# Random features in row and column groups, local layers by slots of both key tiles, offsets on VectorE

## The chip, the core and the metric

The kernel runs on one NeuronCore of a Trainium2 chip. TensorE (PE; its weight loads are listed as PEld) multiplies matrices into PSUM, VectorE (DVE), ScalarE (ACT) and GpSimd (POOL) do the work by elements, and SyncE (SP) issues most DMAs. PSUM has eight banks of 128 partitions by 512 f32 values. Every engine takes its instructions in the order in which the program issued them, and waits for the others at semaphores. The metric is the device time of one execution in microseconds (us); less is better.

## The reference

A network of 16 blocks on a stream x of 16 x 256 tokens with 128 channels, all in f32; each block adds its result to x. The change concerns blocks 2, 3 and 4. Blocks 2 and 4 are the same local attention with two layers, block 3 is an attention by random features (a performer). What they compute, with `_layernorm(x)` ahead of each:

```python
# local attention, one of two layers (8 heads of 64, windows of 64 tokens, 341 hidden)
q, k, v = split(shift_token(x) @ wqkv)
q, k = rotary_xpos(l2norm(q) * qs, l2norm(k) * ksc)
mask = (i < j) | (i > j + WINDOW) | (j == -1)
o = softmax(where(mask, -max, 8 * q @ k.T)) @ v
x = x + o @ wo
h = norm(shift_token(x)) * lg + lb
a, g = split(h @ w1 + b1)
x = x + (a * gelu(g)) @ w2 + b2

# performer (16 heads of 8, 32 random features per head)
def phi(u):
    proj = u @ omega.T
    return exp(proj - 0.5 * sum(u * u) - max(proj)) / sqrt(32) + 1e-6
pq, pk = phi(q * 8**-0.25), phi(k * 8**-0.25)
num, den = pq @ (pk.T @ v), pq @ sum(pk)
x = layernorm(x + (num / den) @ wo) * ln1_g + ln1_b
x = layernorm(x + gelu(x @ w1 + b1) @ w2 + b2) * ln2_g + ln2_b
```

## The kernel before

Activations stay in SBUF with channels on the partitions: x, and two work tiles ha and hb, each 128 x 4096. A chunk is 512 tokens (eight chunks), a tile is 128 tokens (32 tiles), and two tiles are one batch of 256 tokens. Steps are written out by hand: a loop over slots calls each step's function for the tile or chunk that is due, and within one engine the instructions stand in the order of these calls. PSUM banks are handed out by tag, with a fixed number for each tag; a new use of a bank waits for the readers of the old one. The helpers mm, act, tt, gt, stt and ts (lines 503 to 543) issue one instruction each, so most rows of the profile carry a helper's line: L504 is a matmul, L508 a transpose, L528 ScalarE, L531, L538 and L543 VectorE, L534 GpSimd. A matmul in f32 is issued as two instructions on TensorE, a transpose as one.

**Local attention, attend** (`local_attend`, line 3360, called once in each of the four local layers). For a tile n, `project` makes q and k in two banks with tag "w" (tokens on the partitions); ScalarE squares both, VectorE multiplies both by tables of cosines and sines into t1 and t2. `rotate` sums the squares by head (VectorE) and adds the halves (GpSimd), `unit` takes the inverse root with a logarithm and an exponential (ScalarE) and multiplies (GpSimd). `turn` transposes to qkt with heads of 64 channels on the partitions and makes v. `score` works on a unit (batch b, half hg of the heads, key tile t): four f32 matmuls with 64 contracted rows into two banks "s". With t = 0 the 192 columns of queries that see the key tile are limited by a minimum against the table "see" (VectorE) and raised in one exponential of 128 x 768; with t = 1 a mask is first put into the banks by a bf16 matmul of the identity (256 columns), and ScalarE raises straight from PSUM. `weigh` follows two units later: twelve f32 matmuls with 32 output rows each, four side by side in the partitions, first the denominators pd (weights are ones) and then the values po, both in banks "o", summed over t. After t = 1 ScalarE makes the inverse rd of pd by a logarithm and an exponential, and `divide` multiplies (VectorE). `out` multiplies a chunk by wo. The banks are w=3, s=2, o=3, and the loop runs over units, two per slot of a tile.

`chunk_steps` adds, by chunk: the norm of x (centre, spread, scale; first layers only, and only for the three chunks that the block before has not normed), `shift` by one token on GpSimd, and the norm of the shifted z in hs, in the banks "w". A norm centres with a matmul (`centre_step`, line 1759: copy by ScalarE, square by GpSimd) and then makes the variance with a second matmul, a logarithm and an exponential (`spread_step`, line 1774). `norm_steps` (line 1791) returns the three steps; with g and b given, the scale step is a multiply on VectorE and an offset on ScalarE (line 1807).

**Local attention, feed-forward** (`local_ffn`, line 3551): for each chunk six wide matmuls with gelu, then three narrow ones; banks f=6, z=2. In the second layer of a block, steps of the next block's norm follow in the banks "z".

**Performer** (`performer_attend`, line 2249; all eight banks have the tag "ps"). `project` makes q and k of a chunk with channels on the partitions, ScalarE scales, GpSimd squares. `lengths` sums the squares by head, `values` makes v. `features` works on a tile: for each of q and k one matmul of 128 x 128 by the block-diagonal w["om"] (128 x 512), a maximum by head and the subtraction on VectorE, one exponential of 128 x 1024 on ScalarE, one scaling on GpSimd. `turn` transposes the features of q, `sums` makes pk.T @ v of a batch and masks it with own and own1, `heads` multiplies a tile (four f32 matmuls of 36 columns), with a reciprocal and a product on VectorE, `join` transposes the result of a chunk back, `out` multiplies by wo and adds, and `end` is the norm with ln1_g and ln1_b. The list `steps` gives each step's slot; a batch passes from features to heads in slots 0 to 5. `performer_ffn` (line 2381) follows, with the second norm.

Of the kernel before, what the change touches and what calls it, by code (L numbers as in the profile page):

```python
# [1649 lines left out]
class Fast(Net):  # L1650
# [140 lines left out]
    def norm_steps(self, pool, src, dst, bank, g=None, b=None, eps="eps5", copy=None, square=False):  # L1791
# [10 lines left out]
        def scale():  # L1802
            if g is None:
                self.tt(dst, dst, held[1], ALU.mult)
            else:
                self.stt(dst, dst, g, held[1], ALU.mult, ALU.mult)
                self.act(dst, dst, AF.Identity, bias=b)
# [441 lines left out]
    def performer_attend(self, w):  # L2249


        nc = self.nc
        h0, y = self.ha, self.hb
        s8 = 8.0**-0.25
        with ExitStack() as st:
            p = self.stage(st, "f2", 1)
            qk, nrm, vs, fs, kvs, fts, os, ots, ends = {}, {}, {}, {}, {}, {}, {}, {}, {}
# [12 lines left out]
            def lengths(c):  # L2270
                pn = self.bank()
                for side in range(2):
                    for t in range(4):
                        at = (2 * t + side) * 16
                        self.mm(pn[:, at : at + 16], qk[c, side][1][:, t * P : t * P + P], w["half"])
                nrm[c] = p.tile([P, 4, 2, 16], F32, tag="nrm", name="nrm", bufs=2)
                nc.vector.tensor_copy(nrm[c].rearrange("p t s h -> p (t s h)"), pn[:, :P])
# [10 lines left out]
            def features(n):  # L2288
                c, t = divmod(n, 4)
                f = p.tile([P, 2, 16, 32], F32, tag="f", name="f", bufs=6)  # L2290
                sub = p.tile([P, 2, 16], F32, tag="sub", name="sub", bufs=2)
                pps = []
                for side in range(2):
                    pp = self.bank()
                    self.mm(pp, qk[c, side][0][:, t * P : t * P + P], w["om"])
                    pps.append(pp.rearrange("p (h m) -> p h m", h=16))
                for side in range(2):
                    nc.vector.tensor_reduce(sub[:, side], pps[side], AX.X, ALU.max)
                self.tt(sub, sub, nrm[c][:, t], ALU.add)
                for side in range(2):  # L2300
                    self.tt(f[:, side], pps[side], sub[:, side, :, None].broadcast_to([P, 16, 32]), ALU.subtract)
                flat = f.rearrange("p s h m -> p (s h m)")
                self.act(flat, flat, AF.Exp)
                nc.gpsimd.tensor_scalar(flat, flat, 32.0**-0.5, 1e-6, ALU.mult, ALU.add)
                fs[n] = f.rearrange("p s h m -> p s (h m)")

            def sums(b):
                pkv = self.bank()
                for g in range(4):
                    for u in range(2):  # L2310
                        n = 2 * b + u
                        self.mm(
                            pkv[:, g * 33 : g * 33 + 33], fs[n][:, 1, g * P : g * P + P], vs[n // 4][:, n % 4, g],
                            start=u == 0, stop=u == 1,
                        )
                kv = p.tile([P, 4, 36], F32, tag="kv", name="kv", bufs=2)
                pk3 = pkv[:, : 4 * 33].rearrange("p (g k) -> p g k", g=4)
                self.tt(kv[:, :, :32], pk3[:, :, :32], w["own"][:, None, :].broadcast_to([P, 4, 32]), ALU.mult)
                self.tt(
                    kv[:, :, 32:], pk3[:, :, 32:33].broadcast_to([P, 4, 4]),  # L2320
                    w["own1"][:, None, :].broadcast_to([P, 4, 4]), ALU.mult,
                )
                kvs[b] = kv

            def turn(n):
                pf = self.bank()
                for g in range(4):
                    self.tr(pf[:, g * P : g * P + P], fs[n][:, 0, g * P : g * P + P])
                ft = p.tile([P, 4, P], F32, tag="ft", name="ft", bufs=3)
                self.act(ft.rearrange("p g t -> p (g t)"), pf, AF.Copy)  # L2330
                fts[n] = ft

            def heads(n):
                ft, kv = fts.pop(n), kvs[n // 2]
                pn = self.bank()
                for g in range(4):
                    self.mm(pn[:, g * 36 : g * 36 + 36], ft[:, g], kv[:, g])
                pn3 = pn[:, :144].rearrange("p (g k) -> p g k", g=4)
                rd = p.tile([P, 4, 4], F32, tag="rd", name="rd", bufs=2)
                nc.vector.reciprocal(rd, pn3[:, :, 32:])  # L2340
                if n % 4 == 0:
                    os[n // 4] = p.tile([P, 4, P], F32, tag="o", name="o", bufs=2)
                self.tt(
                    os[n // 4][:, n % 4].rearrange("p (g h k) -> p g h k", g=4, h=4),
                    pn3[:, :, :32].rearrange("p g (h k) -> p g h k", h=4),
                    rd[:, :, :, None].broadcast_to([P, 4, 4, 8]), ALU.mult,
                )

            def join(c):
                pt = self.bank()  # L2350
                o = os.pop(c)
                for t in range(4):
                    self.tr(pt[:, t * P : t * P + P], o[:, t])
                ots[c] = p.tile([P, CH], F32, tag="ot", name="ot", bufs=1)
                self.act(ots[c], pt, AF.Copy)
# [1452 lines left out]
```

## Time and profile before

Three executions took 4376.58, 4367.05 and 4374.96 us, the median is 4374.96 us. The execution that was profiled is another one.

| what | value |
|---|---|
| profiled execution | 4392.96 us, its span 4391.2 us |
| TensorE busy, mean granted clock | 3966.2 us (90%), 0.952 |
| VectorE, ScalarE, GpSimd busy | 2605.3, 2376.1, 2119.4 us |
| attend of a local layer, first to last score matmul | 140.9 to 417.4, 519.5 to 782.4, 1198.8 to 1475.3, 1577.7 to 1841.0 us |
| performer attend, first to last subtraction of features | 883.1 to 1057.5 us |
| score matmuls (64 rows) | 2048, median 322 ns |
| products with values, with ones (32 columns of the array) | 4096 and 2048, median 300 and 312 ns |

A row of the profile gives the engine, the line, the operation, what is written and what is read, and the shape. In the answers in order of time a row begins with its start and its duration in us, and equal neighbours are merged with their count. A note in square brackets is the idle time of the engine before the row, and what ended it. Durations of matmuls overlap with their neighbours, so what an instruction costs TensorE is read from the distance of two starts.

### The profile page before, as it was taken

How to read it: one execution, taken by the hardware profiler on the slowest of the kernel's cores; microseconds unless marked ns; L12 is line 12 of the kernel's file. 1: busy time of each engine (PE TensorE's matmuls, PEld its weight loads, DVE VectorE, ACT ScalarE, POOL GpSimd, SP SyncE). 2: the span in 40 equal slices, each digit the busy share in tenths (PEclk: the TensorE clock that was granted, in tenths of full speed). 3: DMA queues.
4: the chain of work that ended last, by engine and by line, in shares of the span. 5: the costliest groups of instructions: out<-in, count | busy, mean ns of one | idle time of the engine just before them, and what ended most of it. 6: DMA issues, size and time to landing. Idle time of an engine off the chain costs nothing. (4 is left out here: it accounts for less than half of the span.)

```text
span 4391.2 us, 72802 instructions
## 1 busy us (share of the span) xinstructions
PE 3966.2 (90%) x28390; PEld 2202.4 (50%) x28390; DVE 2605.3 (59%) x4455; ACT 2376.1 (54%) x4549; POOL 2119.4 (48%) x1776
## 2 busy tenths in 40 slices
PE   7899999999899999995989969887999899899978
PEld 3455455466355445543975549643333344355333
DVE  4764566364366377456336643564888788386374
ACT  6665466444766456553447634445555554675442
POOL 4653355232455255315433334466998789521251
PEclk8999999999999999997999979998999999999989
DMA  1800000000000000001940029200000000000000
GB/s 59 332 1 1 11 1 1 19 1 1 19 1 1 1 3 1 1 0 49 310 162 10 15 88 326 86 18 16 1 1 1 3 1 1 15 2 18 6 0 20
DMA packets 78400, 176.36 MB, mean 40 GB/s; under 512 B 12606, under 2 KB 39108, under 8 KB 77920
## 3 DMA queue, kind: packets, MB, share of 16 engines
q1 hardware_dynamic: 65568, 148.40, 9.8%
q0 software_dynamic: 9120, 18.51, 1.2%
q8 instruction: 227, 3.72, 0.4%
q10 hardware_dynamic: 3360, 4.72, 0.3%
q14 instruction: 125, 1.02, 0.1%
HBM read 118.28 MB, written 54.20 MB: 39 GB/s over the span
## 5 line engine op out<-in xcount | busy, mean ns | idle before, releaser
L528 ACT ACTIVATE pt<-ps 128x512 f32<-128x512 f32 (+1 forms) x896 | 423.1, 537 | 408.1 <-PE ps L504 406.8
L504 PE MATMUL ps<-hb,w 128*128 128x512 f32 (+1 forms) x960 | 468.9, 623 | 5.4 <-issue 3.3
L531 DVE TENSOR_TENSOR t<-ps,tab 128x512 f32<-128x512 f32 x512 | 319.3, 683 | 196.1 <-ACT sq L528 191.3
L504 PE MATMUL ps<-w,hb 128*128 128x512 f32 (+2 forms) x896 | 415.1, 576 | 13.6 <-DVE t L531 11.3
L534 POOL TENSOR_TENSOR t<-t,ss 128x1024 f32<-128x1024 f32 x128 | 243.7, 1904 | 306.8 <-ACT ss L528 197.7
L534 POOL TENSOR_TENSOR t<-t,t 128x512 f32<-128x512 f32 x256 | 320.5, 1275 | 13.2 <-PE ps L504 10.1
L504 PEld LDWEIGHTS ps<-hb,w 128*128 128x128 f32 (+1 forms) x960 | 183.6, 196 | 273.5 <-issue 247.3
L531 DVE TENSOR_TENSOR u<-u,ps 128x384 f32<-128x384 f32 (+1 forms) x206 | 121.8, 595 | 277.8 <-ACT u L528 131.2
L534 POOL TENSOR_TENSOR nsq<-ha 128x512 f32<-128x512 f32 x112 | 123.2, 1100 | 314.1 <-ACT ha L528 297.3
L504 PE MATMUL ps<-nsq,ct 128*128 128x512 f32 x368 | 209.5, 654 | 53.9 <-POOL nsq L534 35.0
L528 ACT ACTIVATE pt<-pt 128x768 f32<-128x768 f32 (+1 forms) x160 | 169.5, 1060 | 154.6 <-DVE pt L531 154.6
L2199 POOL DMA_INDIRECT back<-y,x x142 | 139.1, 980 | 184.2 <-ACT y L528 90.2
L504 PE MATMUL ps<-qkt 64*128 64x192 f32 (+1 forms) x2048 | 216.2, 326 | 11.8 <-ACT pt L528 11.8
L504 PE MATMUL ps<-u,w 128*128 128x512 f32 (+1 forms) x448 | 218.8, 612 | 8.0 <-POOL u L534 8.0
L504 PE MATMUL ps<-ot,w 128*128 128x512 f32 x448 | 211.1, 604 | 15.2 <-POOL ot L534 6.9
L504 PE MATMUL ps<-xt,w 128*128 128x128 f32 x1704 | 219.8, 279 | 1.5 <-ACT xt L528 1.5
L504 PEld LDWEIGHTS ps<-qkt 64*128 64x128 f32 x2048 | 153.1, 188 | 133.3 <-ACT qkt L528 51.5
L504 PEld LDWEIGHTS ps<-w,hb 128*128 128x128 f32 x896 | 147.4, 192 | 139.4 <-issue 110.7
L531 DVE TENSOR_TENSOR pt<-ps,w 128x384 f32<-128x384 f32 (+1 forms) x320 | 171.2, 576 | 75.6 <-PE ps L504 72.2
L3705 POOL DMA_INDIRECT rows<-out,idx x128 | 126.4, 988 | 174.6 <-ACT out L528 125.6
L528 ACT ACTIVATE u<-ps,w 128x512 f32<-128x512 f32 x160 | 107.2, 685 | 186.3 <-PE ps L504 183.5
L531 DVE TENSOR_TENSOR pt<-pt,w 128x1024 f32<-128x1024 f32 (+1 forms) x96 | 181.1, 1886 | 42.3 <-ACT pt L528 42.3
(362 smaller groups left out, 9127.2 us busy)
## 6 DMA issues: line engine op xcount, KB each, us to landing
w<-in_moe_x SPq DMA_DIRECT2D x142, 533.0 KB
rows<-t SPq DMA_DIRECT2D x64, 520.0 KB
x<-rows SPq DMA_DIRECT2D x142, 65.0 KB
w<-in_local_f SPq DMA_DIRECT2D x8, 659.5 KB
y<-back ACTq DMA_DIRECT2D x16, 256.0 KB
y<-back SPq DMA_DIRECT2D x16, 256.0 KB
w<-in_local_f SPq DMA_DIRECT2D x4, 658.5 KB
back<-y,x POOLq DMA_INDIRECT x142
```

What stands on the lines that cost most here:

```text
L504: self.nc.tensor.matmul(out, lhsT, rhs, start=start, stop=stop)
L528: self.nc.scalar.activation(out, in_, func, **kw)
L531: self.nc.vector.tensor_tensor(out, a, b, op)
L534: self.nc.gpsimd.tensor_tensor(out, a, b, op)
L2199: nc.gpsimd.indirect_dma_start(views[i], bass.IndirectOffsetOnAxis(ap=x[:, C : C + 1].bitcast(I32), axis=0), y, None, bounds_check=2 * NT ...
L3705: nc.gpsimd.indirect_dma_start(views[(c * 2 + k) * 4 + t], bass.IndirectOffsetOnAxis(ap=idx[:, k, t : t + 1], axis=0), out[:, k, t], None,)
```

## The change

**Offsets.** The scale step of `norm_steps` adds b with a tensor_scalar on VectorE in place of an activation on ScalarE. It concerns the two norms of the performer, 16 instructions in all; the local layers get steps of their own, `norm_of_half`, with four steps and the offset still on ScalarE.

**Performer.** `features` works on a batch: 16 f32 matmuls of 32 rows by 128 columns, each with the four heads of one group g, into four banks with the tag "f"; the maxima of two groups, an addition and two subtractions follow, twice. `raised` is a step of its own, one slot later. `sums` makes the denominators 32 wide too, `heads` works on a batch with the features as the moving operand and 32 output rows for each group, so that `join` falls away; the reciprocal becomes a logarithm and an exponential on ScalarE. Banks are f=4, ps=4, and a batch passes from features to heads in slots 0 to 7.

**Local attend.** A slot m is a batch and a half of the heads, with both key tiles. `score` takes four banks "s": four bf16 masks of 128 columns, then the products of t = 0 and t = 1 without a change of kind between them; the 128 columns per head of t = 1 lie in a second tile pu. The last two of these are raised in `score`, the first two and the 768 columns in `first_weights`, after `turn`. `weigh` follows one slot later, values first and denominators last; the denominators lie in the upper half of the slot's fourth bank. The banks are w=3, s=4, o=1. Tiles are turned two slots ahead of their score and projected five slots ahead.

**Local feed-forward.** The norm of the last chunk moves from the end of attend into the first four chunks of `local_ffn`, with the table of the logarithm loaded before its spread step.

```diff
@@ norm_steps
-                self.act(dst, dst, AF.Identity, bias=b)
+                self.ts(dst, dst, b, ALU.add)
@@ performer_attend
+            def features(b):
...
+                pps = [self.bank("f") for _ in range(4)]
+                for u in range(2):
+                    for side in range(2):
+                        for g in range(4):
+                            rows, t = slice(32 * g, 32 * g + 32), b % 2 * 2 + u
+                            self.mm(
+                                pps[g][:, (2 * u + side) * P : (2 * u + side) * P + P],
+                                qk[c, side][0][rows, t * P : t * P + P], w["om"][rows, g * P : g * P + P],
+                            )
+                for k in range(2):
+                    gs = slice(2 * k, 2 * k + 2)
+                    for g in (2 * k, 2 * k + 1):
+                        nc.vector.tensor_reduce(sub[:, g], pps[g].rearrange("p (n m) -> p n m", m=32), AX.X, ALU.max)
+                    flat = sub[:, gs].rearrange("p g n -> p (g n)")
+                    self.tt(flat, flat, nrm[c][:, b % 2, 32 * k : 32 * k + 32], ALU.add)
+                    for g in (2 * k, 2 * k + 1):
+                        self.tt(
...
+                        )
+            def raised(b):
+                for k in range(2):
+                    flat = fs[b][:, 2 * k : 2 * k + 2].rearrange("p g u s m -> p (g u s m)")
+                    self.act(flat, flat, AF.Exp)
+                    nc.gpsimd.tensor_scalar(flat, flat, 32.0**-0.5, 1e-6, ALU.mult, ALU.add)
...
+            def heads(b):
+                ft, kv = fts.pop(b), kvs.pop(b)
                 pn = self.bank()
...
+                for k in range(2):
+                    for g in range(4):
+                        nc.tensor.matmul(pn[32 * g : 32 * g + 32, k * T : k * T + T], kv[:, k, g], ft[:, g], start=k == 0, stop=k == 1, skip_group_check=True)
+                rd = p.tile([P, T], F32, tag="rd", name="rd", bufs=2)
+                self.act(rd, pn[:, T:], AF.Ln)
+                self.act(rd, rd, AF.Exp, scale=-1.0)
...
+                self.tt(ots[b // 2][:, b % 2 * T : b % 2 * T + T], pn[:, :T], rd, ALU.mult)
...
+                (13, 4, NCH, end(2)), (12, 4, NCH, end(1)), (11, 4, NCH, end(0)), (10, 4, NCH, out),
+                (7, 2, B, heads), (5, 2, B, sums), (3, 1, NTILE, turn), (1, 2, B, raised), (0, 2, B, features),
...
+            with self.share(f=4, ps=4):
+                self.tiles_in_slots(-7, NTILE + 14, steps)
@@ local_attend
+            def score(m):
...
+                ps = [self.bank("s") for _ in range(4)]
+                for x in (*(b[:, 384:] for b in ps[:2]), *(b[:, :P] for b in ps[2:])):
+                    self.mm(x, identb, masked, stop=False)
...
+                for i, t, bank, at in ((0, 0, 0, 0), (1, 0, 0, 192), (0, 1, 0, 384), (1, 1, 2, 0)):
                     for a in range(2):
...
+                        product(a, i, t, ps[bank + a][:, at : at + 192 - 64 * t])
...
+                for a in range(2):
+                    self.act(pu[:, 2 + a], ps[2 + a][:, :P], AF.Exp)
+                weights[m] = pt, pu
+                spare[:] = ps
+
+            def first_weights(m):
+                pt, pu = weights[m]
+                for a in range(2):
+                    self.act(pu[:, a], spare[a][:, 384:], AF.Exp)
+                flat = pt.rearrange("p a t -> p (a t)")
+                self.act(flat, flat, AF.Exp)
+
+            def weigh(m):
...
+                pd, po = spare[3][:, T:] if m < NTILE - 1 else self.bank("s")[:, T:], self.bank("o")
+                pt, pu = weights.pop(m)
+                for half in (0, 1, -1):
+                    for t in range(2):
...
+            with self.share(w=3, s=4, o=1), self.tc.manual_schedule():
                 self.logs()
...
+                for m in range(-9, NTILE + 6):
+                    if within(m, NTILE):
+                        score(m)
+                    if within(m - 1, NTILE):
+                        weigh(m - 1)
+                    c, rest = divmod(m - 5, 4)
+                    if rest == 0 and 0 <= c < NCH:
                         out(c)
...
+                    if within(m + 2, NTILE):
+                        turn(m + 2)
+                    if within(m, NTILE):
+                        first_weights(m)
+                    if within(m + 4, NTILE):
+                        rotate(m + 4)
+                    if within(m - 1, NTILE):
+                        inverse(m - 1)
+                        divide(m - 1)
+                    if within(m + 4, NTILE):
+                        unit(m + 4)
+                    chunk_steps(m)
+                    if within(m + 5, NTILE):
+                        project(m + 5)
@@ local_ffn
+                end = self.norm_of_half(p, "z", w, hn[:, self.chunk(NCH - 1)])
                 for k in range(NCH + 1 + len(lead)):
                     if k < NCH:
                         wide(k)
+                    if k < 4:
+                        if k == 1:
+                            self.logs(False)
+                        end[k]()
                     if 0 < k <= NCH:
                         narrow(k - 1)
```

## The prediction

> **What bounds the kernel now.** I read the busy table first, then the slices of the span, then the order of instructions in time inside each stage that the change touches. The page's first rows:
>
> ```profile
> span 4391.2 us, 72802 instructions
> PE 3966.2 (90%) x28390; PEld 2202.4 (50%) x28390; DVE 2605.3 (59%) x4455; ACT 2376.1 (54%) x4549; POOL 2119.4 (48%) x1776
> ```
>
> TensorE is busy nine tenths of the span. Asked for the stretches: attend of the second local layer (497 to 785 us) 275.8 of 288 us, performer attend (868 to 1083 us) 204 of 215. What matters is therefore the spacing of TensorE's starts. One tile step of local attend, TensorE alone in order of time (start, duration, instruction, count):
>
> ```profile
> 263.24 0.92 PE L504 MATMUL ps<-qkt 64*128 64x192 f32 x8
> 264.09 0.53 PE L3478 MATMUL ps<-pt,ct 128*32 128x192 f32 x8
> 264.44 0.83 PE L3478 MATMUL ps<-pt,v 128*32 128x192 f32 x16
> 265.20 1.98 PE L504 MATMUL ps<-w,hb 128*128 128x512 f32 x4
> 267.02 1.02 PE L504 MATMUL ps<-hb,ct 128*128 128x512 f32 x2
> 267.88 0.38 PE L504 MATMUL ps<-masked,identb 128*128 128x256 bf16 x2
> 268.19 0.71 PE L504 MATMUL ps<-qkt 64*128 64x128 f32 x8
> 268.84 0.42 PE L3478 MATMUL ps<-pt,ct 128*32 128x128 f32 x8
> 269.08 0.62 PE L3478 MATMUL ps<-pt,v 128*32 128x128 f32 x16
> 269.63 1.09 PE L508 MATMUL ps<-ct,t 128*128 128x128 f32 x8
> 270.56 1.02 PE L504 MATMUL ps<-w,hb 128*128 128x512 f32 x2
> ```
>
> No row carries an idle note. Differences of starts: scores 0.85, sums 0.35, values 0.76, projection 1.82, centring 0.86, mask 0.31, scores 0.65, sums 0.24, values 0.55, transposes 0.93, v 0.96 us: 8.28 with the norm's matmul, 7.42 without. A 512-column f32 instruction costs 0.427 us in a run, 128 columns 0.107. At that pace the rows (pairs of 64-row and fours of 32-column tiles together) add up to 6.3 us; the other 1.1 us lies where tile shapes change: about 0.1 into the 64-row scores, 0.2 out of them, 0.12 out of the 32-column products.
>
> Where TensorE does wait: the end of each local attend, and the norm of x in a first layer (three chunks):
>
> ```profile
> 785.54 1.98 PE L504 MATMUL ps<-ot,w 128*128 128x512 f32 x4
> 788.13 1.98 PE L504 MATMUL ps<-ot,w 128*128 128x512 f32 x4 [0.61 <-DVE ot L531]
> 792.34 1.21 PE L504 MATMUL ps<-hb,ct 128*128 128x512 f32 x2 [2.23 <-POOL hb L696]
> 795.36 2.07 PE L504 MATMUL ps<-nsq,ct 128*128 128x512 f32 x2 [1.81 <-POOL nsq L534]
> 797.22 3.30 PE L504 MATMUL ps<-hb,w 128*128 128x512 f32 x4
> ```
>
> ```profile
> 251.36 1.10 PE L504 MATMUL ps<-nsq,ct 128*128 128x512 f32 x2 [2.42 <-ACT qkt L528]
> ```
>
> [...]
>
> **Local attend, a full slot (128 of them: 32 in each of 4 layers).** Six changes of tile shape become three. Masks: four of 128 columns for two of 256; loads paced at 0.1, so about 0.5 for 0.31. Scores 0.64+0.43+0.21 = 1.28 for 1.50. Products 1.60+0.15 = 1.75 for 1.90. Transposes 0.93. v 0.86 and projection 1.76, no longer followed or preceded by a change, for 2.78. Sum 7.08 for 7.42.
>
> But with all four "s" banks taken by every slot, the next slot's fourth mask needs the bank whose upper half holds the denominators, so it waits for their logarithm. In the changed order of ScalarE that stands behind the copy of v, two 128-column exponentials and the 768-column one. Counted from the start of the v matmul, with paces from ScalarE's rows in time (copy starts 1.07 later and takes 0.50, exponentials 0.16 each, worked out from 0.28 for two of 256 columns, 768 columns 0.76, logarithm 0.39, hand-over 0.1): the fourth mask can go at 3.22, the next v at 3.22+0.1+1.28+1.75+0.93 = 7.3 (R1). Behind that mask stand the scores and products, and VectorE's minima and ScalarE's exponentials wait for those. TensorE alone would be there at 7.08. A second chain (R2): after the logarithm its exponential, the two of the unit norm, the slot's norm work on ScalarE, the two squares, then the exponential of the denominators' bank, before the sums: 6.75 plus the norm work. A third (R3): first square, four VectorE multiplies (2.48), which free the bank of the next v: 7.0 plus the norm work. Behind those multiplies VectorE has the minima of the next scores (1.02 for two), which ScalarE wants only 1.6 us after the next v has begun.
>
> Norm work is 0.6 (offset), 0 plus centring 0.5, 1.2 (spread), 0 over four slots; TensorE gets 0.86 in the second and third and the output product (3.5) in the fourth. Four slots after: 7.6, 7.94, 8.2, 7.3+3.5: 34.5. Before: 4 x 7.42 + 1.72 + 3.54 = 34.9. So the steady part gains only 0.4 in four slots.
>
> **A whole layer.** From first to last score before: 519.48 to 778.73, 259.25 us. After: six early slots without norms 47.3 (five of 7.3, one 10.8), five fours 172.5, the last ones without a projection 26.0 (R1 holds them at 7.3 where before takes 5.6 from start to start), edges 9.9: 255.7, gain 3.5. Filling: before, three tiles must be turned ahead of the first score, after two; GpSimd hands out one per 4.5 us (its unit products end at 504.4, 509.0, 514.7): gain 3.5. End: from the last score to the first feed-forward matmul 18.5 us before; after, 1.8 + 1.75 + 0.86 + 1.75 + 1.71 + 0.1 + 1.71 = 9.7, less 0.3 that starts early, plus 1.8 of centring and spreading that now run in the feed-forward: 11.2, gain 7.3. There the last chunk's norm is covered by wide() (69.0 of 69 us busy on TensorE, ScalarE 38.6; two table loads of 1.28 and 1.9 of work fit); uncovered it would be the 5.8 us of before. Sum 14.3 a layer, 57 for four. In the two first layers the 2.42 stall goes three times (the square is ready a slot earlier), and a new one of 1.15 comes: the second projection waits for the bank of x's centring, copied late on ScalarE. Net 6 each, 12. I take 0.1 us per slot off (13) for hand-overs that I don't see: local layers **56** us.
>
> **Performer attend.** 11.3 us per batch before (features' subtracts from 883.1 to 1057.5 for 32 tiles). Features: eight 512-column instructions, 3.44; after 32 of 32 rows x 128 columns in four row groups. Bounds: 0.85 (four together) to 3.4 (loads one after the other); I take 1.7, the two-group pace. Heads: 16 instructions of 36 columns, 1.62, become 16 of 256 in fours, 1.0; the transposes of join (0.22 per batch) go; two shape changes add 0.4. So TensorE falls to about 9.9. The new wait: all four "f" banks are held until VectorE has subtracted (5.74 for reduces, adds, subtracts), and in every other batch the next transposes wait for a copy of q behind the exponentials: 6.1 + 1.06 + 0.6 + 0.1 + 0.5 + 1.7 = 10.1. Gain about 1.2 x 15.5 = 19, and 4 at the end, where reciprocal, product and join become one logarithm and one product: **23** us. Other pieces (a second masked product of 0.22 per batch, a logarithm and an exponential of 0.39 and 0.42) lie in idle time of VectorE (127 of 215 us busy) and ScalarE (91).
>
> **Offsets and DMAs.** No DMA is added or moved. 16 offsets of 0.72 on ScalarE become 16 on VectorE. No such form is in the trace (nearest 0.74 from PSUM; 128 columns 0.22); 0.2 to 0.75. Covered by matmuls in both stages but for the last ones: 1 us, from -1 to +1 open.
>
> **Sum.** 56 + 23 + 1 = 80. The profiled execution took 4392.96 (span 4391.2 and 1.8 around it), so 4313; the runs' median, 4374.96, is 0.4% below it: **4295 us**.
>
> **Rivals.** (1) ScalarE's chain runs at durations, not paces: R1 and R2 grow by 0.43, four slots by 1.3, times 32: 42 lost, 4337. For: ScalarE was busy for 182.6 of 288 us and gets 0.45 per slot more (four of 0.28 for two of 0.33). Against: back-to-back copies run at 0.49, not 0.60. (2) The feature loads do not overlap: 3.4 instead of 1.7, performer loses 5 where it gained 23: 4323. For: the loads are 128 columns wide whatever the rows; against: the 64-row rows. (3) Slower: R3 is the bound. If VectorE's multiplies stand at 0.68 each rather than 0.62, the chain runs at durations, and one more hand-over of 0.1 is met, a slot costs 0.7 more, 128 x 0.7 = 90: 4385. It decides from 0.63 us per slot on (80/128). For: v waits for that bank in every slot of the changed order; against: the four multiplies take 2.48 in each row. (4) The shape changes do not shrink with their number and everything else holds: 0.3 per slot, still 4335.
>
> **Chances.** Forecast 0.54 (4265 to 4325); (1) and (4) 0.22; (2) 0.10; (3) 0.14. Left out, together under two in ten: the half of (3) above 4385 and a forecast that fell below 4250 because the slots ran at TensorE's 7.08. Within 0.2% (9 us), about what runs of this kernel can tell from no change, lies only the overlap of (1) and (3). Faster 0.82, same 0.04, slower 0.14.
>
> **What would show it.** In the changed profile: starts of v 7.3 to 8.2 us apart in slots without the output product; the fourth mask waiting for "rd" by 0.2 to 0.4 us in slots without a norm matmul; no wait of 2 us between output product and feed-forward; features' subtracts about 10 us apart per batch; no table load between scores. Wrong: idle notes above 0.7 us in every slot (behind DVE t or ACT pu), or performer attend above 215 us.

## The result and the profile after

The changed kernel takes 4302.59 us (median of four, 4300.0 to 4305.64) against 4375.77 us before: ratio 0.9836, 95% interval 0.9819 to 0.9853, so 64 to 79 us faster. The forecast of 4295 has the right sign and lies 7.6 us below the median. Of its three parts one came out near the forecast, and two were wrong by large factors in opposite directions.

The first rows of the changed kernel's page:

```profile
span 4301.6 us, 74012 instructions
PE 3881.4 (90%) x28998; PEld 2210.2 (51%) x28998; DVE 2620.8 (61%) x4423; ACT 2369.4 (55%) x4821; POOL 2123.8 (49%) x1776
```

The busy share of TensorE is 90% as before. The two profiled spans differ by 89.6 us, and 19.6 of these lie behind the last stage that the change touches, where the code is the same: in the execution of before TensorE waited 9.9 us at one place for VectorE's routing. The stages must therefore be compared one by one, each from its first matmul to that of the next (in us):

| stage | before | after | difference |
|---|---|---|---|
| local attend, four layers: first projection to first score | 99.1 | 95.7 | -3.5 |
| the same: first to last score group | 1077.5 | 1045.1 | -32.3 |
| the same: last score group to feed-forward | 61.6 | 44.4 | -17.2 |
| local feed-forward, four layers | 272.1 | 274.3 | +2.2 |
| performer attend | 212.8 | 200.9 | -11.9 |
| performer feed-forward with its norms | 90.2 | 84.6 | -5.7 |

These sum to 68.4. (The prediction counts the last score of before from 778.73 us, a score group 3.25 us ahead of the last one; in its terms 13 us move from the second row to the third.) The start of the first local layer moved by another 1.6 us; over the runs below it lies between 112.7 and 118.5 us, before anything that the edits touch.

One slot of local attend after, TensorE alone in order of time (start, duration, instruction, count), with the last rows taken from narrow windows around the masks of the next slot:

```profile
522.26 0.69 PE L504 MATMUL ps<-masked,identb 128*128 128x128 bf16 x4
522.88 1.36 PE L3452 MATMUL ps<-qkt 64*128 64x192 f32 x16
524.17 0.53 PE L3492 MATMUL ps<-pt,v 128*32 128x192 f32 x8
...
525.94 1.09 PE L508 MATMUL ps<-ct,t 128*128 128x128 f32 x8
526.87 2.74 PE L504 MATMUL ps<-w,hb 128*128 128x512 f32 x6
529.45 0.33 PE L504 MATMUL ps<-masked,identb 128*128 128x128 bf16 x3
529.92 0.22 PE L504 MATMUL ps<-masked,identb 128*128 128x128 bf16 x1
```

From mask to mask it is 7.19 us. Masks to scores take 0.62; in the slots with a norm's matmul it is 0.32. The difference, 0.30, is the fourth mask: it starts at 529.92, 0.14 after the end of the third, where its neighbours overlap. No idle note shows so short a gap: equal neighbours are merged across it. ScalarE in order of time names what it waits for, the logarithm of the denominators, which ends at 529.87:

```profile
529.47 0.40 ACT L528 ACTIVATE rd<-ps 128x256 f32<-128x256 f32 x1
```

The end of the second layer's attend and, from the first layer, the places that answer to the stall of 2.42:

```profile
761.84 1.13 PE L504 MATMUL ps<-nsq,ct 128*128 128x512 f32 x2
763.58 0.53 PE L3492 MATMUL ps<-pt,v 128*32 128x192 f32 x8 [0.62 <-DVE ot L531]
...
765.35 3.73 PE L504 MATMUL ps<-ot,w 128*128 128x512 f32 x8
769.86 2.41 PE L504 MATMUL ps<-hb,w 128*128 128x512 f32 x5 [0.78 <-DVE ha L531]
```

```profile
233.75 1.13 PE L504 MATMUL ps<-w,hb 128*128 128x512 f32 x2 [0.74 <-ACT ha L528]
258.32 0.66 PE L508 MATMUL ps<-ct,t 128*128 128x128 f32 x4 [0.54 <-DVE t L531]
```

No wait above 0.8 us is left at the end; the feed-forward starts behind the output product, after 0.78.

In the performer the picture is worse than forecast. TensorE of before, two rows, and TensorE and VectorE of the changed kernel at the start of chunk 6, each in order of time:

```profile
899.01 1.88 PE L504 MATMUL ps<-w,q 128*128 128x512 f32 x4
900.73 0.98 PE L504 MATMUL ps<-kv,ft 128*128 128x36 f32 x8
```

```profile
955.63 0.63 PE L508 MATMUL ps<-ct,f 128*128 128x128 f32 x4
959.65 3.75 PE L504 MATMUL ps<-ha,w 128*128 128x512 f32 x4 [3.39 <-ACT f L528]
963.20 1.91 PE L504 MATMUL ps<-x,ct 128*128 128x512 f32 x2
964.90 1.49 PE L504 MATMUL ps<-ot,w 128*128 128x512 f32 x2
966.23 0.60 PE L508 MATMUL ps<-ct,f 128*128 128x128 f32 x4
966.76 1.17 PE L504 MATMUL ps<-w,q 32*128 32x128 f32 x32
967.86 0.38 PE L504 MATMUL ps<-w,ha 128*128 128x128 f32 x1
```

```profile
957.28 1.29 DVE L531 TENSOR_TENSOR f<-ps,sub 128x512 f32<-128x512 f32 x2
958.48 1.02 DVE L531 TENSOR_TENSOR ha<-ha,nrs 128x512 f32<-128x512 f32 x1
```

Three things are to be seen. The features' products of a batch take 1.10 us (966.76 to 967.86), where two tiles of before took 2 x 1.72. q and k wait 3.39 us, three times in the stage; the note names ScalarE's exponential, but on VectorE the scaling of x, which q and k read, stands behind the subtractions of the features and ends at 959.5. And the four instructions behind the wait take 3.55 us, from 959.65 to 963.20, where four of 512 columns took 1.72 above: TensorE runs at half speed. The granted clock is 0.50 from 959.02 to 965.83.

Half speed comes without a wait too. Busy times by engine, with the granted clock in the third number from the end, of before (889 to 908 us, chunk 1) and of after (870 to 889 us, chunk 2):

```profile
889.00:908.00 19.00, 18.94 (x116) 14.09 (x115) 12.80 (x30) 6.21 (x10) 5.68 (x7) 1.00 0.01 1
```

```profile
870.00:889.00 19.00, 19.00 (x171) 14.01 (x170) 11.61 (x25) 9.34 (x15) 6.29 (x7) 0.72 0.00 1
```

TensorE is busy for all but 0.06 us of both stretches, at a clock of 1.00 in one and 0.72 in the other. The busy share does not show this.

### The profile page after: what moved, and what is told of

Read it like the earlier page. It is cut to its first block, busy times and chain, and to the rows that moved or that the text cites. A ratio compares the mean times of both kernels' runs of the same rounds, so it can differ in the third digit from the quotient of the medians.

```text
span 4301.6 us, 74012 instructions
## 1 busy us (share of the span) xinstructions
PE 3881.4 (90%) x28998; PEld 2210.2 (51%) x28998; DVE 2620.8 (61%) x4423; ACT 2369.4 (55%) x4821; POOL 2123.8 (49%) x1776
## 5 line engine op out<-in xcount | busy, mean ns | idle before, releaser
L528 ACT ACTIVATE pt<-ps 128x512 f32<-128x512 f32 x640 | 339.7, 600 | 314.4 <-PE ps L504 313.1
L504 PE MATMUL ps<-w,hb 128*128 128x512 f32 (+2 forms) x896 | 405.5, 574 | 26.3 <-DVE t L531 20.4
L528 ACT ACTIVATE qkt<-ps 128x512 f32<-128x512 f32 x256 | 140.5, 595 | 309.6 <-PE ps L508 309.0
L531 DVE TENSOR_TENSOR ot<-ps,rd 128x512 f32<-128x512 f32 (+2 forms) x224 | 143.1, 639 | 254.3 <-ACT rd L528 254.3
L504 PEld LDWEIGHTS ps<-w,hb 128*128 128x128 f32 x896 | 156.3, 193 | 184.4 <-issue 115.0
L504 PEld LDWEIGHTS ps<-xt,w 128*128 128x128 f32 x1704 | 204.8, 194 | 2.9 <-ACT xt L528 2.9
L528 ACT ACTIVATE nrs<-ps,ct 128x512 f32<-128x512 f32 x208 | 139.8, 684 | 98.9 <-PE ps L504 93.1
```

Source lines behind the costliest of these rows:

```text
L504: self.nc.tensor.matmul(out, lhsT, rhs, start=start, stop=stop)
L528: self.nc.scalar.activation(out, in_, func, **kw)
L531: self.nc.vector.tensor_tensor(out, a, b, op)
```

## The experiments

The kernel before ran beside each group of these runs, with medians from 4373.5 to 4375.7 us; beside the run called denser it took 4394.0, so ratios are compared there. A stage's length and clock come from one profiled execution of each kernel.

**Each half alone.** The change is taken apart by function.

```diff
 # performer alone: performer_attend (features, raised, sums, heads, slots, f=4, ps=4) as after
-                self.ts(dst, dst, b, ALU.add)
+                self.act(dst, dst, AF.Identity, bias=b)
 # local_attend and local_ffn as before
 # local layers alone: local_attend and local_ffn as after, performer_attend as before,
 # and the offset on ScalarE here too
```

> The kernel before with the performer's change alone (features, raised, sums, heads, slots, banks); local layers and offsets as before. The prediction as written: 23 us less than before, about 4353. From the traces of before and after (performer attend 212.8 us against 200.9, its feed-forward and the norms after it 90.2 against 84.5, of which the change can own little): 12 to 17 us less, about 4361. If the missing ten lie in an interplay with the changed local layers, this run shows the full 23; if they lie inside the performer, the stage takes about 201 us here too, with three waits of 3.4 us ahead of q and k of the last chunks.

> The kernel before with the local layers' change alone (attend by slots of both key tiles, last norm moved into the feed-forward); performer and offsets as before. The prediction as written: 56 us less, about 4320. From the traces: the four attends lose 14.9, 11.4, 13.3 and 13.5 us and the feed-forwards gain 0.4 to 0.8 each, 51 less, about 4325. The rival that a slot is bound by ScalarE's or VectorE's chain would show starts of the projection more than 7.5 us apart in slots without norm or output; TensorE-bound slots stand 7.2 to 7.4 apart.

The local layers alone: 4315.98 us, ratio 0.9871 (0.9855 to 0.9888), 57.5 us less than before, where 56 was forecast. The performer alone: 4370.0, ratio 0.9992 (0.9986 to 0.9999), 3.5 us less, where 23 was forecast. Its stage takes 205.5 us, with the waits ahead of q and k of 3 us, so the missing part lies inside the performer. The two add up to 61 of 73; the offsets are the next piece.

**Offsets back on ScalarE.**

```diff
-                self.ts(dst, dst, b, ALU.add)
+                self.act(dst, dst, AF.Identity, bias=b)
```

> The changed kernel with the 16 offsets of the performer's two norms back on ScalarE. The prediction as written: 1 us more, from 1 less to 1 more, since the offsets lie under matmuls: about 4303. The rival that the last runs suggest: performer change alone is worth 4 us, together with the local layers' and the offsets' 71 of which the local layers own 57, so 8 to 10 are left for the offsets: 4311 to 4313, with 4 of them in the stretch from the performer's feed-forward to the next projection (84.55 after, 88 to 90 where the offset is on ScalarE) and 4 in the attend (200.9 after, 205.5).

4310.1 us, ratio 0.9861 (0.9842 to 0.9879): 7.5 more than the changed kernel. The intervals overlap, so the size is uncertain, but the stages repeat those of the performer alone, which has the offset on ScalarE too: attend 205.43 (after 200.92), feed-forward with norms 88.02 (after 84.55). The reason in the second is in ScalarE's order of time at the end of that feed-forward:

```profile
1135.26 0.63 ACT L528 ACTIVATE nrs<-nrs 128x512 f32<-128x512 f32 x1
1135.80 0.58 ACT L528 ACTIVATE ha<-ps 128x512 f32<-128x512 f32 x1
1136.28 0.71 ACT L528 ACTIVATE ha<-ha,w 128x512 f32<-128x512 f32 x1
1137.00 1.28 ACT L1662 ACT_TABLE_LOAD   x1
```

ScalarE goes from norm to norm with a table load of 1.28 us each and has no idle note from 1109 to 1144 us, while TensorE, from 1127 on, waits 0.6 to 2.0 us ahead of each norm's second matmul. Five offsets of 0.71 stand in that chain: 3.5 us. VectorE, which has gaps of 1 to 3 us there, does one in 0.49 to 1.15.

**The norm of the last chunk back at the end of attend.**

```diff
-                    if (c := due(6 + i)) is not None and c < NCH - 1:
+                    if (c := due(6 + i)) is not None:
 # local_ffn:
-                end = self.norm_of_half(p, "z", w, hn[:, self.chunk(NCH - 1)])
...
-                    if k < 4:
-                        if k == 1:
-                            self.logs(False)
-                        end[k]()
```

> The changed kernel with the norm of the last chunk back at the end of each local attend, out of the feed-forward. The prediction's price of the uncovered norm is 5.8 us for each of four layers, less 1.7 of TensorE time that leaves the feed-forward: 4 x 4.1 = 16 us more, 4319. If a cold clock at the start of the feed-forward comes with it (the feed-forward before began with 24 matmuls in 11.9 us where 10.3 is the pace), another 1 to 1.5 per layer: 4324. If the norm was covered before as well, nothing: 4303.

4321.4 us, ratio 0.9882 (0.9866 to 0.9899), 18.8 more. Each end grows from 11.1 to 17.1 to 17.3 us, by 6.2 where 5.8 was the price, and each feed-forward shrinks by 0.8 to 1.3. The move is worth what it was said to be worth. In this run the performer's attend, whose instructions are those of the changed kernel, took 191.8 us instead of 200.9; the clock was 0.88 instead of 0.83. This execution, 4306.68 us, was the fastest of its kernel, the others took 4320.34 to 4325.2. In chunk 2, busy times and clock as above:

```profile
875.57:890.95 15.38, 15.27 (x174) 12.07 (x173) 13.79 (x28) 9.22 (x15) 6.28 (x7) 1.00 0.01 2
```

The same 174 instructions run at the full clock here and take 15.4 us from q to q, where the changed kernel took 19.3 at a clock of 0.73. So the instructions alone do not settle the clock. That spread belongs to every comparison of this stage below.

**Two more changes of tile shape in a slot.**

```diff
-                for x in (*(b[:, 384:] for b in ps[:2]), *(b[:, :P] for b in ps[2:])):
-                    self.mm(x, identb, masked, stop=False)
+                for b2 in ps[:2]:
+                    self.mm(b2[:, 384:], identb, masked, stop=False)
 # ahead of the last pair of products of t = 1:
+                    if bank:
+                        for b2 in ps[2:]:
+                            self.mm(b2[:, :P], identb, masked, stop=False)
```

> The changed kernel with the masks of a slot's third and fourth bank put between its score products instead of ahead of all of them: the same instructions, but two more changes of TensorE's tile shape (64 rows to 128 and back) in each of 128 slots. The prediction's prices, 0.1 into the 64-row products and 0.2 out of them, give 0.3 x 128 = 38 us if slots are bound by TensorE: 4341. If a chain on ScalarE or VectorE bounds a slot, as the prediction said of the fourth mask, the extra 0.3 is swallowed: 4303 to 4310. Slots without norm or output stand 7.19 apart after; they should stand 7.5 apart in the first case.

TensorE of this kernel in order of time, the masks and scores of one slot:

```profile
526.01 0.27 PE L504 MATMUL ps<-masked,identb 128*128 128x128 bf16 x2
526.22 1.14 PE L3452 MATMUL ps<-qkt 64*128 64x192 f32 x12
527.29 0.28 PE L504 MATMUL ps<-masked,identb 128*128 128x128 bf16 x2
527.51 0.49 PE L3452 MATMUL ps<-qkt 64*128 64x128 f32 x4
```

Up to the first product with v at 527.93, masks and scores take 1.92 us (0.32 + 1.29 = 1.61 in the changed kernel where nothing waits), so the price of 0.3 for a pair of changes is right. Yet the kernel takes 4305.17 us (0.9836, 0.9821 to 0.9851), and a slot without norm or output stays at 7.19: the 0.3 is swallowed by the wait of the fourth mask, which these slots no longer show. Of the steady four only one, with a norm's matmul, grows (7.75 to 8.05); the other three stay within 0.01. The plain slots are bound by ScalarE's chain to the logarithm, 0.3 above the 6.89 of the one plain slot in which no mask waits.

**The features' products over 128 rows.**

```diff
-                                qk[c, side][0][rows, t * P : t * P + P], w["om"][rows, g * P : g * P + P],
+                                qk[c, side][0][:, t * P : t * P + P], w["om"][:, g * P : g * P + P],
```

> The changed kernel with the features' products over all 128 rows of the block-diagonal table instead of 32 rows in four groups, into the same banks: 32 instructions of 128 columns, 0.107 each, 3.4 us per batch where the trace shows 1.10. If TensorE's work bounds the stage, 16 x 2.3 = 37 us more, 4340. If VectorE's chain (5.74 of reduces and subtractions per batch) and the waits bound it, under 10 more. If the dense work also keeps the clock up (0.83 in this stage after, 0.94 before), the loss shrinks by up to 20 us: 4310 to 4320, with a granted clock above 0.9.

4321.1 us, ratio 0.9882 (0.9865 to 0.9898), 18.5 more; the stage grows by 22.2, and its clock is 0.92; the time lies about midway between the two plain answers. To part work, waits and clock I take each stage's length, the sum of TensorE's idle notes in it, and the granted clock; (1 - clock) x length is the time lost to the clock, and the remainder is TensorE's own work (in us; the clock has two digits, so the last two columns are good to 1; a wait at the half clock is counted in both columns, which makes 2.9 us in the changed kernel and 4.8 at most):

| performer attend in | length | waits | clock | lost to clock | own work |
|---|---|---|---|---|---|
| before | 212.8 | 10.7 | 0.94 | 12.8 | 189 |
| local layers alone | 210.5 | 12.1 | 0.96 | 8.4 | 190 |
| performer alone | 205.5 | 31.6 | 0.84 | 32.9 | 141 |
| offsets on ScalarE | 205.4 | 31.6 | 0.84 | 32.9 | 141 |
| changed kernel | 200.9 | 24.7 | 0.83 | 34.2 | 142 |
| end norm back | 191.8 | 26.3 | 0.88 | 23.0 | 143 |
| masks in two groups | 200.3 | 25.0 | 0.83 | 34.1 | 141 |
| features over 128 rows | 223.1 | 21.0 | 0.92 | 17.8 | 184 |
| first wait filled | 199.4 | 15.8 | 0.85 | 29.9 | 154 |
| all slots moved | 199.9 | 18.1 | 0.81 | 38.0 | 144 |
| scale earlier | 192.7 | 21.4 | 0.86 | 27.0 | 144 |
| scale earlier, again | 192.7 | 20.1 | 0.85 | 28.9 | 144 |
| waits filled | 188.2 | 13.9 | 0.90 | 18.8 | 155 |
| denser | 188.8 | 13.6 | 0.95 | 9.4 | 166 |

The own work comes out the same, within 3 us, for kernels with the same instructions in this stage. The change cut it by 47 us, and 35 came back: 14 as waits and 21 as clock. Of the three executions with the changed kernel's stage two lost 34 us to the clock and one 23. Over 128 rows 42 us of work are added and 16 of clock are won back.

**The scale step of x one slot earlier.**

```diff
-                (-4, 4, NCH, norm(2)), (-6, 4, NCH, norm(1)), (-7, 4, NCH, norm(0)),
+                (-5, 4, NCH, norm(2)), (-6, 4, NCH, norm(1)), (-7, 4, NCH, norm(0)),
```

> The changed kernel with one number changed: the scale step of x's norm in the performer one slot earlier, where VectorE has no subtractions of features ahead of it. If the three waits of 3.39 us ahead of q and k come from that place in VectorE's order, they go: at least 3 x 3.4 = 10 us less, and up to 20 if TensorE's clock, which falls to half for 3.4 to 6.8 us after each of them, stays up: 4283 to 4292. If q and k really wait for ScalarE's exponential of the features, which the trace names, nothing changes: 4303.

> The kernel with the scale of x one slot earlier once more, beside the next one: 4290 again, the performer's attend 190 to 195 us.

4289.99 us, ratio 0.9807 (0.979 to 0.9823), and again 4288.59, 0.9808 (0.9795 to 0.9821): 13 to 14 less than the changed kernel. Its nine executions took 4280.8 to 4293.9 us, the changed kernel's four 4300.0 to 4305.6. The stage alone would not tell: it took 192.7 us both times, and 191.8 to 200.9 where it was not edited. The three waits of 3.39 are gone, so VectorE's order made them and not the exponential that the note named. Waits of 2.0 to 2.1 us ahead of the centring of x show up in their place, and the last two chunks take 21.1 us each, from q to q, instead of 23.7 to 27.0 in three executions of the unedited stage.

**Waits filled with matmuls.** First in the changed kernel, then on top of the earlier scale.

```diff
 # project, in the changed kernel:
+                    if c >= 5 and not side:
+                        for _ in range(4):
+                            self.mm(pq, w[wn], h0[:, : CH])
                     self.mm(pq, w[wn], h0[:, s])
 # out and end, with the earlier scale:
+                for _ in range({4: 3, 5: 4, 7: 2}.get(c, 0)):
+                    self.mm(ph, w["wo"], h0[:, :CH])
                 self.mm(ph, w["wo"], ots.pop(c))
+                    if c == 7 and i == 1:
+                        pd = self.bank()
+                        for _ in range(2):
+                            self.mm(pd, w["wo"], h0[:, :CH])
```

> The changed kernel with eight more matmul instructions of 512 columns (four products, 3.4 us, whose result is overwritten) ahead of q in the last three chunks of the performer, where TensorE waits 3.39 us for the scaled x. They only fill the wait and keep TensorE at work. If idle windows cost the clock and the clock costs time, q, k and what follows run at full speed after the fill: the rows of q and k, 3.5 us for four at half speed, take 1.7, and 2 to 4 us per chunk are gained: 4291 to 4297. If the wait alone matters, the time stays at 4303; if the fill only adds work, up to 10 more.

> The kernel with the scale one slot earlier, and 22 more matmul instructions of 512 columns (0.43 us each), whose results are overwritten or never read, in four waits of the performer's attend: ahead of the output product of chunks 4, 5 and 7 (waits of 2.4, 4.2 and 2.2 us) and ahead of the last norm's second matmul (1.8). They add 9.4 us of TensorE work, all in waits. If the halved clock behind those waits costs time, 14 us of rows at half speed run at full speed and 5 to 8 us are gained: 4282 to 4285, and the granted clock of the stage rises from 0.86 to 0.9 or more. If only the waits count, 4290; if the fill does not fit, up to 9 more.

The first gave 4298.92 us (0.9823, 0.9803 to 0.9843), 3.7 less, with overlapping intervals. The waits of the stage fell from 24.7 to 15.8 us with 10.2 us of matmuls added (24 of 0.427), but chunks 1 and 2, which the edit doesn't touch, had more of the half clock than before (21 us each instead of 19.5; the run with the masks in two groups has the same 21 there), and the stage's clock is 0.85. Taken alone this is inconclusive.

The second gave 4285.18 us (0.9793, 0.9779 to 0.9806), the fastest of all, 3.4 below the kernel without the fill beside it, again with overlapping intervals. The stage fell from 192.7 to 188.2 us with 9.4 us of matmuls more in it:

```profile
839.98:1028.18 188.20, 173.94 (x1459) 118.75 (x1458) 125.58 (x245) 94.19 (x152) 65.24 (x68) 0.90 0.03 12
```

Most of that is not the fill's doing: the last centring of x, which stands ahead of the first fill, starts 113.1 us into the stage instead of 116.3, after the same instructions. From there to the feed-forward it is 75.1 us instead of 76.4 (76.5 in the first run with the earlier scale), and 73.5 in the run below, which has the fill too, so the fill pays for itself and gains 1.3 to 2.9. The output product of chunk 5 in order of time, without the fill and with it:

```profile
1000.46 2.08 PE L504 MATMUL ps<-ot,w 128*128 128x512 f32 x2 [4.15 <-DVE ot L531]
1002.32 1.06 PE L508 MATMUL ps<-ct,f 128*128 128x128 f32 x4
```

```profile
999.73 1.13 PE L504 MATMUL ps<-ot,w 128*128 128x512 f32 x2 [0.72 <-DVE ot L531]
1000.69 0.60 PE L508 MATMUL ps<-ct,f 128*128 128x128 f32 x4
```

Behind the filled wait the two products take 0.96 from start to start instead of 1.86, and the transposes 0.53 instead of 0.99. The half speed behind this wait is gone; in the changed kernel, where nothing fills it, the clock behind it was 0.50 from 1010.22 to 1017.03.

**Denser where nothing waits.**

```diff
 # lengths, on top of the last kernel:
+                for _ in range(2 if 1 <= c <= 3 else 0):
+                    self.mm(pn, w["wo"], h0[:, :CH])
 # sums:
+                if b < 4:
+                    self.mm(pkv, w["wo"], h0[:, :CH])
```

> The kernel with the waits filled, and 20 more instructions of 512 columns whose results are overwritten, in places where TensorE does not wait: two products ahead of the sums of squares of chunks 1 to 3 and one ahead of each of the first four batches' sums with v. They add 8.5 us of work among products of 16, 33 and 128 columns. If thin products alone, without a wait, make the clock fall (it stood at half for 20 us between 16 and 47 us of the stage in the last run), that time at half speed goes, 10 us are won back, and the stage takes 186 to 190 us instead of 188.2. If only waits make it fall, it stays, and the stage takes 197: the time then is 4294 instead of 4285.

4309.77 us against 4394.0 for before beside it: ratio 0.9808 (0.9792 to 0.9824) where the last kernel had 0.9793. The intervals overlap; taken by itself the time lies nearer to the answer that nothing is won back. The stage of the profiled execution says otherwise: busy times by engine, clock third from the end,

```profile
842.86:1031.64 188.78, 174.82 (x1479) 115.70 (x1478) 125.48 (x245) 93.98 (x152) 65.25 (x68) 0.95 0.03 12
```

With 20 instructions more (8.5 us) the stage takes 188.8 instead of 188.2 us, the waits are the same (13.6 and 13.9), and the clock rose from 0.90 to 0.95. The last centring of x starts 115.3 us into it, with 8.5 us of work added ahead, against 113.1 and 116.3 without. That fits thin products that lower the clock without a wait, but it is one execution, and the rise is no larger than the spread of 0.05 between executions of equal code above; that the density did it is not shown.

**All slots around the norms moved.**

```diff
-                (13, 4, NCH, end(2)), (12, 4, NCH, end(1)), (11, 4, NCH, end(0)), (10, 4, NCH, out),
+                (14, 4, NCH, end(2)), (13, 4, NCH, end(1)), (12, 4, NCH, end(0)), (11, 4, NCH, out),
-                (-4, 4, NCH, norm(2)), (-6, 4, NCH, norm(1)), (-7, 4, NCH, norm(0)),
+                (-5, 4, NCH, norm(2)), (-6, 4, NCH, norm(1)), (-8, 4, NCH, norm(0)),
...
-                self.tiles_in_slots(-7, NTILE + 14, steps)
+                self.tiles_in_slots(-8, NTILE + 14, steps)
```

> The changed kernel with the performer's slots moved: scale of x one earlier, centring of x one earlier (it waits 2.1 us for the bank of q in the same slot), output product and the norm after it one later (it waits 2.2 to 4.2 us for VectorE's product of the same batch). The scale alone gave 12.6. If the other waits are real too (6.2 and 9.2 us in that run), they go in part: 8 to 12 us more, 4278 to 4282. If the waits only move to VectorE's queue, which is busy 124 of 192 us, 4290.

4299.79 us, ratio 0.9837 (0.9819 to 0.9856): the gain of the earlier scale is lost again. The waits fell a little (18.1 us in the stage; 20.1 with the earlier scale alone), the clock fell to 0.81, and from the last q and k to the feed-forward it is 63.8 us instead of 59.4, since the last output product and norm come a slot later. Why the clock is lower here was not settled.

## Why the prediction was right, and where it was wrong

**Local layers, 56 forecast, 57.5 measured alone (51 in the stages of the changed kernel).** The mechanism of a plain slot held. R1 is the bound of plain slots at 7.19 us (7.3 forecast), with the wait of the fourth mask at 0.30 (0.2 to 0.4 forecast) and TensorE's own 6.89 (7.08). (The terms shown for 3.22 add up to 3.14; the trace has 3.05.) The steady four slots of the second layers take 34.35 (34.5), though one by one they take 8.42, 7.75, 7.34 and 10.84 where 7.6, 7.94, 8.2 and 10.8 were forecast. The end's norm is worth 6.2 (5.8).

The other terms were off and cancelled in part, which is luck. The four slots of before take 36.0 us, not 34.9: in the slot with the output product the scores wait 0.84, which that sum left out.

```profile
591.23 1.19 PE L504 MATMUL ps<-qkt 64*128 64x192 f32 x8 [0.84 <-ACT pt L528]
```

So the fours gained more than 8 us per layer instead of 2, and the slots around them lost 5 where 1.5 was to be gained; from first to last score 3.6 came out beside 3.5. In the first layers the stall of 2.42 is gone; in its place come 0.74 for the bank of x's centring, three times a layer where 1.15 was counted once, and two of 0.54 each time, not foreseen: 1.8 us net per layer instead of 6. Filling the first layer of slots was to gain 3.5 per layer and gained 0.9 (3.5 in all instead of 14): GpSimd's 4.5 us per tile is not the only limit, and a fill waits for VectorE's products (2.71 us ahead of 487.73) and ScalarE's copies (1.83 ahead of 492.23) as well, with rows at half speed in it (six instructions from 493.13 take 5.1 us, at a clock of 0.50, where 2.6 is the pace). Against that, first to last score, end and feed-forward together gained 47 where the forecast's terms give 55, and 42 with the 13 us taken off for hand-overs: that reserve was larger than what the waits of the first layers took.

**Performer, 23 forecast, 3.5 measured alone, 12 in the stage of the changed kernel.** The failed step is "Features: ... I take 1.7, the two-group pace" followed by "TensorE falls to about 9.9 ... 10.1". The features take 1.10 us per batch, not 1.7. The sum has an error as well: its listed terms (1.74, 0.62 and 0.22 saved, 0.4 added) leave 9.1 of 11.3, not 9.9, that is 35 us in 16 batches. With 1.10 in place of 1.7 they give 44, near the 47 by which TensorE's own work fell. The forecast did not rest on this, since it took the wait for the banks, 10.1, as the bound. It then stopped at TensorE's work and the banks; it had no term for VectorE's order, where a longer block of 5.7 us now stands ahead of x's scale, and none for the clock, where thin products replaced dense ones. Together 35 us came back, and the spacing of subtractions was 7.4 to 15.0 us per batch and 11.0 on average, not about 10; before it was 11.2.

**Offsets, 1 forecast, 7.5 measured.** The failed step is "Covered by matmuls in both stages but for the last ones". Under matmuls says nothing where ScalarE's own chain with its table loads sets the end; 3.5 us of it is shown above. The other 4.5 lie in the attend. That is within the spread of this stage, but its waits are 31.6 us in both executions with the offset on ScalarE and 24.7 to 26.3 in the three with it on VectorE; which of them is due to which instruction was not followed further.

So 80 was forecast and 73 came, because the offsets, forecast at 1 us, made up for a part of the performer. That the total came so near is luck. The three pieces measured apart add to 68.5; the remaining 5 is within their intervals and within the 9 us by which the performer's stage differs between two runs with the same code in it.

**The rivals.** (1), ScalarE's chain at durations, would have made four slots 1.3 longer: refuted by 34.35. (2), no overlap of the features' loads: refuted by 1.10 us for 32 instructions, 0.034 each, where it asks for 3.4. (3), VectorE's multiplies and the bank of v as the bound: refuted, v has no idle note in the steady slots of the second layers, and four of them take 34.35, where it asks for 2.8 more. (4), shape changes that don't shrink: refuted by the price of 0.3 for a pair. The four chances add up to 1 and leave no room for the cases named as left out.

**The clock.** In the changed kernel it fell to 0.50 toward the end of each of the three waits of 3.39 us and of the one of 4.15, 0.3 to 1.2 us before TensorE started again, and stood there from 931.70 to 938.52, 959.02 to 965.83, 986.33 to 989.72 and 1010.22 to 1017.03 us. But it fell without a wait too: from 880.51 to 887.32 TensorE was busy 6.81 of 6.81 us at 0.50, in the stretch ahead, 873.70 to 880.50, 6.80 of 6.80 at 1.00. Over the stage the clock stood at 0.94 and 0.96 in the two kernels with the old stage, at 0.81 to 0.88 wherever the thinner products came without filling, and at 0.92 with the features over 128 rows, so the new stage costs clock, by its thinner products, its waits or both; but in chunk 2 the same instructions ran at 0.73, 0.66 and 1.00. What makes the clock fall was not shown: the busy table does not tell it, and which property of the thin products matters (rows, columns, loads, or the transposes among them) was not separated.

## What to carry over

When a change makes matmuls thinner, cost the clock as a term of its own: take length, idle notes and granted clock of the stage, and expect part of the saved work back (here 35 of 47 us). One execution is not enough for such a stage: its clock varied by 0.05 and its length by 9 us with the same instructions. When one engine's instructions are gathered into larger blocks, look for the small step of another stage that is now queued behind the block, and who reads its result; moving that step by one slot was worth 13 us here. An operation "under matmuls" was not free here where its own engine had no gaps: the offsets on ScalarE, forecast at 1 us, cost 7.5.

## What was not expected of the hardware

Sixteen f32 products (32 instructions) of 32 rows and 128 columns in four row groups took 1.10 us, 34 ns each, and their 32 weight loads 0.98 us beside them: near the prediction's estimate of 0.85 (32 x 0.107 over four), far from the 3.4 of one after the other. The performer's attend with identical code ran 191.8, 200.3 and 200.9 us long, with a clock of 0.88, 0.83 and 0.83. And 18 us of added matmuls, 9.4 in waits and 8.5 outside them, did not lengthen that stage: it took 188.8 us, and 192.7 twice without them.
